# Eight weight-sum jobs moved from batch 1's first passes to batch 0's, the last four token blocks routed singly, and a third buffer for slots and pairs

## The chip, the cores and the metric

The kernel runs on one core of a Trainium2 chip. The metric is the device time of one execution in microseconds (us). The engines are TensorE (PE in the profile; PEld is its weight load), VectorE (DVE), ScalarE (ACT), GpSimd (POOL) and SyncE (SP). GpSimd and SyncE issue the DMAs; each engine works through its own instructions in order.

## The reference

One block of a transformer with modulated norms, on 2 batches of 4096 tokens with 512 channels, in float32: linear attention with 16 heads of 32, then a mixture of 8 experts, of which each token takes 2.

```python
h = layernorm(x) * (1 + ca) + sa
# linear attention: q, k = relu(h @ wq), relu(h @ wk); v with a row of ones
vk  = einsum('bhen,bhdn->bhed', v_pad, k)
out = einsum('bhed,bhdn->bhen', vk, q);  out = out[:-1] / (out[-1:] + EPS)
x = x + ga * (out @ w_proj.T + b_proj)
h = layernorm(x) * (1 + cb) + sb
# experts: top 2 of 8 by softmax of a router; each token's rows are sorted by expert
act = gelu(h_sorted @ w_gate[:, 0]) * (h_sorted @ w_gate[:, 1])
x = x + gb * sum_over_2(weight * (act @ w_linear) * per_expert_scale)
```

## The kernel before, in words

Tokens are worked in blocks of 512 (`TB`), eight per batch, sixteen in all (`order`). There are three stages.

**First passes** (`firsts`, `first`, L907 and L492). For each block the tokens are normed and transposed (`prepare`), then TensorE makes k (`pk`, L500), q (`pq`, L517) and the sum over tokens of k with the normed x (`pa`, L537). VectorE takes each result out of PSUM (L505, L523, L544). The q rows go to DRAM.

**Second passes** (`seconds`, `merge`, `attend`, `second_norm`, L951 on). When a batch's sums are whole, `merge` folds values and projection into one matrix. Then each block reads its q rows back, is divided, transposed and projected (`po`, L682), and normed again (L728, L732). A routed group follows with `route` (L761): VectorE picks the two experts of each token, counts ranks and writes two small tiles, `pair` (token number and weight) and `slot` (the row of the map). GpSimd then scatters them into `map_d` in DRAM, one indirect DMA for 128 tokens and one choice (L887): 16 for a group of two blocks, 8 for one block. `group_of` says which blocks are routed together: two at a time, the last two alone.

**Experts** (L1403 on). Seven products take the place of eight in the big units (`seven`, L1190), for which sums of quarter blocks of the expert weights are wanted beside the weights. The first map fetch (`fetch_map`, L1120) waits for all scatters.

These weight sums are made by the generator `weight_sums` (L419): 24 jobs, two gate halves and one linear weight for each of 8 experts. Each job has four parts:

```python
raw = big(f"wraw_{n}")
nc.gpsimd.dma_start(out=raw..., in_=src)          # L431: 1 MB in, GpSimd's queue
nc.vector.tensor_tensor(to, one, two, op)         # L446: four sums on VectorE
nc.gpsimd.dma_start(out=dst, in_=new...)          # L447: 1 MB out, GpSimd's queue
```

`raw` and `new` are taken from the tag `big`, which has five buffers and is shared with xT of the blocks, h2, and the weights of `merge`.

How the two streams run is written out by hand. All of batch 0's first passes go alone. Then batch 1's first passes and the second passes alternate, six steps of a second pass for each block with two of a first pass behind each. What is left of the second passes goes alone at the end. The framework (Tile) places the instructions on the engines from this order and sets the waits.

Of the kernel before, what the change touches and what calls it, by code (L numbers as in the profile page):

```python
# [10 lines left out]
I32 = mybir.dt.int32  # L11
# [6 lines left out]
P = 128  # L18
B, N, C = 2, 4096, 512
HEADS, HD = 16, 32  # L20
E, TOPK, H = 8, 2, 512
# [7 lines left out]
NBLK = N // TB  # L29
# [21 lines left out]
def adaln_linear_attention_moe_kernel(  # L51
# [81 lines left out]
    with ExitStack() as st:  # L133
# [39 lines left out]
        def load_mod(m):  # L173
            wm = big(f"wm_{m}")
            nc.sync.dma_start(out=wm, in_=chunks(wmod[:, m * C : (m + 1) * C]))
            wm_of[m] = wm
# [39 lines left out]
        def mod_columns(m):  # L216
            wm = wm_of.pop(m)
            pc = bank(f"pmc_{m}")
            for g in range(KC):
                for k in range(KC):  # L220
                    nc.tensor.matmul(
                        pc[:, g * B : (g + 1) * B],
                        wm[:, k, g * P : (g + 1) * P],
                        silu[:, k, :],
                        start=(k == 0), stop=(k == KC - 1),
                    )
            nc.vector.tensor_scalar(
                modc[:, m].rearrange("p k b -> p (k b)"), pc[:, 0 : KC * B],
                float(m == 1), None, ALU.add,
            )  # L230
# [138 lines left out]
        def load_wot():  # L369
            wot_of.append(big("wot"))  # L370
            nc.sync.dma_start(out=wot_of[0], in_=chunks(wprojt))
# [47 lines left out]
        def weight_sums():  # L419

            jobs = []
            for e in range(E):
                rows = slice(e * P, (e + 1) * P)
                for m in range(2):
                    src = wgate[rows, m * 4 * KH * QN : (m + 1) * 4 * KH * QN]
                    r0 = (2 * e + m) * P
                    jobs.append((src, wgsum_d[r0 : r0 + P, :], True))
                jobs.append((wlin[rows, :], wlsum_d[rows, :], False))
            for n, (src, dst, left) in enumerate(jobs):
                raw = big(f"wraw_{n}")  # L430
                nc.gpsimd.dma_start(out=raw.rearrange("p q n -> p (q n)"), in_=src)  # L431
                new = big(f"wnew_{n}")
                a, b, c, d = (raw[:, q, :] for q in range(4))
                s = [new[:, q, :] for q in range(4)]
                if left:
                    steps = (
                        (s[0], d, c, ALU.add), (s[1], s[0], a, ALU.subtract),
                        (s[2], a, d, ALU.subtract), (s[3], b, s[1], ALU.subtract),
                    )
                else:  # L440
                    steps = (
                        (s[0], d, a, ALU.subtract), (s[1], c, s[0], ALU.subtract),
                        (s[2], c, d, ALU.subtract), (s[3], b, s[1], ALU.subtract),
                    )
                for to, one, two, op in steps:
                    nc.vector.tensor_tensor(to, one, two, op)  # L446
                nc.gpsimd.dma_start(out=dst, in_=new.rearrange("p q n -> p (q n)"))  # L447
                yield
# [10 lines left out]
        def prepare(b, i):  # L459

            if (b, i) not in xin:
                load_x(b, i)
            xt = xin[(b, i)]
            name = f"{b}_{i}"
            s6 = sm.tile([P, NT, nc.vector.BN_STATS_DIM], FP, tag="bn6", name=f"bn6_{name}")
            mv = sm.tile([P, NT, 2], FP, tag="mv", name=f"mv_{name}", bufs=4)
            dev = sm.tile([P, NT], FP, tag="dev", name=f"dev_{name}", bufs=4)
            for t in range(NT):
                nc.vector.bn_stats(s6[:, t, :], xt[:, t, :])
                nc.vector.bn_aggr(mv[:, t, :], s6[:, t, :])  # L470
            nc.scalar.activation(dev, mv[:, :, 1], AF.Sqrt, bias=eps_ln)
            nc.vector.reciprocal(mv[:, :, 1], dev)
            t0 = (b * NBLK + i) * NT
            nc.vector.tensor_scalar(xl[:, t0 : t0 + NT, E], mv[:, :, 0], -1.0, None, ALU.mult)
            xh = []
            for t in range(NT):
                h = row("xh", f"xh_{b}_{i}_{t}", 8)
                nc.vector.tensor_scalar(
                    h, xt[:, t, :], mv[:, t, 0:1], mv[:, t, 1:2], ALU.subtract, ALU.mult
                )  # L480
                xh.append(h)
            xT = big(f"xT_{b}_{i}")
            for k in range(KC):
                pt = ps_t.tile([P, 512], FP, tag="tr", name=f"pt_{b}_{i}_{k}")
                for t in range(NT):
                    nc.tensor.transpose(  # L486
                        pt[:, t * P : (t + 1) * P], xh[t][:, k * P : (k + 1) * P], ident
                    )
                nc.scalar.copy(xT[:, k, :], pt)
            prepared[(b, i)] = (xh, xT, dev)  # L490
# [270 lines left out]
        def route(b, group, lm, rq, ssq):  # L761
            blk, nt = group[0], len(group) * NT

            def tl(shape, tag, bufs=1, dt=FP):

                n = 1
                for s in shape[1:]:
                    n *= s
                t = sm.tile([P, n * 2 * NT // nt], dt, tag=tag, name=f"{tag}_{blk}", bufs=bufs)
                t = t[:, 0:n]  # L770
                if len(shape) == 3:
                    return t.rearrange("p (a b) -> p a b", a=shape[1])
                if len(shape) == 4:
                    return t.rearrange("p (a b c) -> p a b c", a=shape[1], b=shape[2])
                return t
# [66 lines left out]
            def chosen(src, tag):  # L842

                prod = tl([P, TOPK, nt * E], "prod")
                nc.vector.tensor_tensor(
                    prod, src, oh.rearrange("p k t e -> p k (t e)"), ALU.mult
                )
                got = tl([P, TOPK, nt], tag)
                nc.vector.tensor_reduce(
                    got, prod.rearrange("p k (t e) -> p k t e", t=nt), AX.X, ALU.add  # L850
                )
                return got

            def over_k(a):
                return a.unsqueeze(1).to_broadcast([P, TOPK, nt * E])
# [18 lines left out]
            nc.vector.tensor_tensor(  # L874
                pk, pk, ren.unsqueeze(1).to_broadcast([P, TOPK, nt]), ALU.mult
            )
            pair = tl([P, TOPK, nt, 2], "pair", 2)
            nc.vector.tensor_tensor(pair[:, :, :, 1], pk, sc, ALU.mult)
            nc.vector.tensor_scalar(
                pair[:, :, :, 0].bitcast(I32), iota_tok[:, :, 0:nt], float(blk * TB), None, ALU.add  # L880
            )
            rank = chosen(over_k(prk), "rank")
            slot = tl([P, TOPK, nt], "slot", 2, I32)
            nc.vector.scalar_tensor_tensor(slot, idx, float(CAP), rank, ALU.mult, ALU.add)  # L884
            for k in range(TOPK):
                for t in range(nt):
# [12 lines left out]
        order = [(b, i) for b in range(B) for i in range(NBLK)]  # L899

        group_of = {}
        for n in range(len(order)):
            alone = n >= len(order) - 2
            group_of[n] = [n] if alone else [n - n % 2, n - n % 2 + 1]
        sums = {}

        def firsts():  # L907

            wsums = weight_sums()
            prepare(0, 0)  # L910
            load_mod(2)
            mod_columns(0)
            load_mod(3)
            mod_columns(1)
            load_mod(5)
            bias_row(0)
            scaled(0, 0)
            for n, (b, i) in enumerate(order):
                if i == 0:
                    sums[b] = (  # L920
                        wp.tile([P, KC, C], FP, tag="acc", name=f"acc_{b}"),
                        wp.tile([P, C], FP, tag="ksum", name=f"ksum_{b}"),
                    )
                steps = first(b, i, *sums[b])
                if n == 0:
                    for _ in range(NT):
                        next(steps)
                        yield
                    bias_row(1)
                    scaled(0, C)  # L930
                    mod_row(4)
                    load_wot()
                    router_columns()
                    for _ in range(NT):
                        next(steps)
                        yield
                    later_rows()
                if n + 1 < len(order):
                    prepare(*order[n + 1])
                if n == 0:  # L940
                    padding()
                if n == 1:
                    for at in (0, C):
                        scaled(1, at)
                for _ in range(2 if b == 0 else 1):
                    next(wsums, None)
                yield from steps

# [539 lines left out]
```

## Time and profile before

| | us |
|---|---|
| median of 3 runs | 2479.77 (2474.09 to 2483.15) |
| profiled execution | 2461.66 |
| its span, first to last instruction | 2459.8 |
| TensorE busy | 2320.4 (94%) |
| VectorE busy | 1466.9 (60%) |
| GpSimd busy | 768.7 (31%) |
| ScalarE busy | 508.7 (21%) |

In the profiled execution batch 0's first passes end at about 416 us, batch 1's at about 927, the last second pass and the routing at about 1135; the experts take the rest. In rows of the profile, "L887" is a line of the kernel, the name after the operation is the tile that is written and behind the arrow what is read. In a timeline the first number is the start, the second the duration, "x8" the number of instructions put together, and the brackets hold the idle time of the engine ahead of the row and what ended it.

### The profile page before, as it was taken

Reading aid. Unit: us, or ns where it says so; the run is one execution under the profiler, and the core shown is the slowest. Engines: PE = TensorE matmul, PEld = TensorE weight load, DVE = VectorE, ACT = ScalarE, POOL = GpSimd, SP = SyncE. Lnnn points to the kernel's source line nnn. Section 1 sums busy time; section 2 is a strip of 40 time slices with the busy share of each in tenths; the row PEclk is TensorE's granted clock in tenths of the full one; section 3 lists DMA queues with packets and bytes.
Section 4 is the critical chain, followed back from the end, with each engine's and each line's share of the span. In section 5 each row is a group of like instructions: output and inputs, shape, how many; then the busy total and the mean of one; then the engine's idle time right before and its main releaser. Section 6 shows DMA issues by size and latency. Waiting matters only on the chain.

```text
span 2459.8 us, 25373 instructions
## 1 busy us (share of the span) xinstructions
PE 2320.4 (94%) x9440; PEld 1681.5 (68%) x9440; DVE 1466.9 (60%) x2895; ACT 508.7 (21%) x1015; POOL 768.7 (31%) x723
## 2 busy tenths in 40 slices
PE   8999999999797999983899999999999999999996
PEld 4565565666464667762777778777887788877884
DVE  3464646666464647994565655655655566655663
ACT  1121211223122323551111111111111111111110
POOL 0100000001102020546544444444544445444431
PEclk9999999999898999996999999999999999999998
DMA  5674544343534534875777777777777777777753
GB/s 210 246 272 145 205 159 159 131 165 116 137 137 125 189 98 126 222 206 167 247 233 240 218 247 231 230 243 254 208 227 234 247 244 213 232 255 222 244 157 66
DMA packets 111728, 486.22 MB, mean 198 GB/s; under 512 B 18593, under 2 KB 18593, under 8 KB 77938
## 3 DMA queue, kind: packets, MB, share of 16 engines
q0 software_dynamic: 71584, 347.12, 45.0%
q1 hardware_dynamic: 40018, 137.44, 17.3%
q8 instruction: 76, 1.25, 0.2%
q14 instruction: 50, 0.41, 0.1%
HBM read 355.63 MB, written 128.88 MB: 197 GB/s over the span
## 4 chain that ended last, share of the span: by engine, by line
PE 83%; DMA 6%; DVE 5%; POOL 4%; issue 2%; ACT 0%; SPq 0%; POOLq 0%; DVEq 0%; ACTq 0%
PE p_g L1200 24%; PE p_l L1200 12%; PE pq L517 9%; PE pgs L1354 8%; PE pa L537 8%; PE pk L500 7%; PE po L682 5%; PE py L1380 4%; POOL map_d L887 3%; DMA map_d<-pair,slot 2%; PE px L1263 2%; DMA x<-in_x 1%; PE pt L486 1%; DMA wraw<-in_wgate 1%; PE pqt L670 1%
## 5 line engine op out<-in xcount | busy, mean ns | idle before, releaser
L1200 PE MATMUL p_g<-xT,wg 128*128 128x256 f32 x1600 | 371.9, 381 | 0.0
L1200 PEld LDWEIGHTS p_g<-xT,wg 128*128 128x128 f32 x1600 | 303.4, 191 | 41.6 <-issue 1.9
L1200 PE MATMUL p_g<-xS,wg 128*128 128x256 f32 x1200 | 283.7, 379 | 0.3 <-DVE xS L1272 0.3
L500 PE MATMUL pk<-wqk,xT 128*128 128x512 f32 x512 | 234.2, 605 | 36.7 <-DVE k L505 36.7
L1200 PEld LDWEIGHTS p_g<-xS,wg 128*128 128x128 f32 x1200 | 228.2, 190 | 31.7 <-DVE xS L1272 1.0
L682 PE MATMUL po<-gm,qT 128*128 128x265 f32 (+1 forms) x1024 | 240.6, 386 | 9.3 <-ACT qT L674 9.3
L517 PE MATMUL pq<-wqk,xT 128*128 128x264 f32 (+1 forms) x1024 | 231.8, 386 | 1.6 <-DVE den L658 1.6
L537 PE MATMUL pa<-k,xh 128*128 128x512 f32 x512 | 225.2, 595 | 0.3 <-DVE acc L544 0.3
L887 POOL DMA_INDIRECT map_d<-pair,slot x128 | 134.2, 1048 | 289.9 <-DVE slot L884 249.1
L517 PEld LDWEIGHTS pq<-wqk,xT 128*128 128x128 f32 x1024 | 195.7, 192 | 37.9 <-issue 4.3
L682 PEld LDWEIGHTS po<-gm,qT 128*128 128x128 f32 x1024 | 189.8, 190 | 44.7 <-ACT qT L674 13.3
L1176 POOL DMA_INDIRECT out<-y_b,mp x100 | 158.1, 1581 | 175.8 <-DVE y_b L1173 152.9
L1354 PE MATMUL pgs<-wgs,xTs 128*128 128x512 f32 x464 | 205.0, 595 | 0.0
L1200 PE MATMUL p_l<-wl,aT 128*128 128x256 f32 x800 | 193.9, 379 | 0.0
L500 PEld LDWEIGHTS pk<-wqk,xT 128*128 128x128 f32 x512 | 95.5, 194 | 142.3 <-issue 100.4
L537 PEld LDWEIGHTS pa<-k,xh 128*128 128x128 f32 x512 | 97.4, 191 | 112.7 <-issue 110.5
L1354 PEld LDWEIGHTS pgs<-wgs,xTs 128*128 128x128 f32 x464 | 88.6, 191 | 111.2 <-issue 109.7
L1200 PEld LDWEIGHTS p_l<-wl,aT 128*128 128x128 f32 x800 | 148.0, 190 | 18.2 <-issue 0.5
L1113 POOL DMA_INDIRECT xg<-h_d,mp x129 | 131.8, 1022 | 71.4 <-issue 34.4
L1292 ACT ACTIVATE ge<-quar_g 128x512 f32<-128x512 f32 x100 | 62.9, 629 | 408.0 <-DVE quar_g L1208 408.0
L1200 PE MATMUL p_l<-wl,aS 128*128 128x256 f32 x600 | 141.8, 379 | 0.0
L1208 DVE TENSOR_TENSOR quar_g<-part_g,p_g 128x512 f32<-128x512 f32 x150 | 102.8, 685 | 53.7 <-PE p_g L1200 51.9
(267 smaller groups left out, 3000.6 us busy)
## 6 DMA issues: line engine op xcount, KB each, us to landing
x<-in_x SPq DMA_DIRECT2D x16, 1024.0 KB
q_d<-q SPq DMA_DIRECT2D x64, 256.0 KB
qi<-q_d SPq DMA_DIRECT2D x64, 256.0 KB
wraw<-in_wgate POOLq DMA_DIRECT2D x16, 1024.0 KB, 6.3
xb_d<-x SPq DMA_DIRECT2D x16, 1024.0 KB
wgsum_d<-wnew POOLq DMA_DIRECT2D x16, 1024.0 KB, 5.6
xb<-xb_d SPq DMA_DIRECT2D x16, 1024.0 KB
out<-xb SPq DMA_DIRECT2D x16, 1024.0 KB
```

The source lines that it names most:

```text
L500: nc.tensor.matmul(pk, xT[:, k, t * P : (t + 1) * P], w[:, k, 0:C], start=(k == 0), stop=(k == KC - 1),)
L517: nc.tensor.matmul(pq[:, C // 2 + c0 : C // 2 + c1], xT[:, k, t * P : (t + 1) * P], w[:, k, C + c0 : C + c1], start=(k == 0), stop=(k == K ...
L537: nc.tensor.matmul(pa, xh[t][:, g * P : (g + 1) * P], ks[t], start=(t == 0), stop=(t == NT - 1),)
L682: nc.tensor.matmul(po[:, C // 2 - EX + c0 : C // 2 - EX + c1], qT[:, g * P : (g + 1) * P], gm[:, g, c0:c1], start=(g == 0), stop=(g == KC ...
L887: ins = nc.gpsimd.indirect_dma_start(out=map_d, out_offset=IndirectOffsetOnAxis(ap=slot[:, k, t : t + 1], axis=0), in_=pair[:, k, t, :], i ...
L1113: return nc.gpsimd.indirect_dma_start(out=dst, out_offset=None, in_=src, in_offset=IndirectOffsetOnAxis(ap=ids, axis=0))
L1176: ins = nc.gpsimd.indirect_dma_start(out=out, out_offset=IndirectOffsetOnAxis(ap=token(mp, t), axis=0), in_=y, in_offset=None, compute_op= ...
L1200: nc.tensor.matmul(bank[:, c, :], left(s, c, k), rhs[:, k, :], start=(k == 0), stop=(k == KH - 1),)
L1208: nc.vector.tensor_tensor(r, one, two, ALU.add)
L1292: nc.scalar.activation(ge, g, AF.Gelu_apprx_tanh)
L1354: nc.tensor.matmul(p, xT[:, k, :], wg[:, :, quarters[k // KH], k % KH, :], start=(k == 0), stop=(k == KC - 1),)
L1380: nc.tensor.matmul(p, aT[:, hc, :], wl[:, q, hc % KH, :], start=(hc == 0), stop=(hc == HC - 1))
```

## The change

Three edits. The weight jobs are taken three per block (`3 * E // NBLK`, which is 3) instead of two per block of batch 0 and one per block of batch 1, so that all 24 are issued with batch 0's eight blocks. The last four blocks are routed singly instead of the last two: blocks 12 and 13, one group with 16 scatters before, become two groups with 8 each. And the tiles `pair` and `slot` have three buffers instead of two.

```diff
-            pair = tl([P, TOPK, nt, 2], "pair", 2)
+            pair = tl([P, TOPK, nt, 2], "pair", 3)
...
-            slot = tl([P, TOPK, nt], "slot", 2, I32)
+            slot = tl([P, TOPK, nt], "slot", 3, I32)
...
         for n in range(len(order)):
-            alone = n >= len(order) - 2
+            alone = n >= len(order) - 4
             group_of[n] = [n] if alone else [n - n % 2, n - n % 2 + 1]
...
                 if n == 1:
                     for at in (0, C):
                         scaled(1, at)
-                for _ in range(2 if b == 0 else 1):
+                for _ in range(3 * E // NBLK):
                     next(wsums, None)
                 yield from steps
```

## The prediction

> **What bounds the kernel now.** I read the page first: its busy line and its two rows in 40 slices.
>
> ```profile
> PE 2320.4 (94%) x9440; PEld 1681.5 (68%) x9440; DVE 1466.9 (60%) x2895; ACT 508.7 (21%) x1015; POOL 768.7 (31%) x723
> ...
> PE   8999999999797999983899999999999999999996
> ...
> PEclk9999999999898999996999999999999999999998
> ```
>
> TensorE works 94% of the span, so time is only to be won where its row dips: slice 10, counted from 0 (615 to 676 us), slice 12 (738 to 799), and slice 18 (1107 to 1168), where the routing ends and the experts begin. Each slice is 61.5 us. The granted clock dips there too.
>
> Next I asked who TensorE waits for from 420 to 1140 us, while batch 1's first passes run beside batch 0's second passes (columns: total us, times, longest):
>
> ```profile
> PE pk L500 <- DVE k L505: 32.8, 2, 18.0
> PE prk L835 <- DVE runs L820: 16.2, 2, 14.2
> PE po L682 <- ACT qT L674: 9.3, 14, 1.0
> ```
>
> Two stalls make 32.8 us. The timelines around them (start, duration, engine, line, in brackets the idle time before) name the cause. GpSimd, 620 to 630 us:
>
> ```profile
> 627.81 0.96 POOL L887 DMA_INDIRECT map_d<-pair,slot  x1 [1.33 <-DMA map_d<-pair,slot]
> 629.45 0.58 POOL L431 DMA_DIRECT2D wraw<-in_wgate  x1 [0.68 <-issue]
> ```
>
> VectorE, then TensorE, 636 to 640 us:
>
> ```profile
> 637.20 1.29 DVE L446 TENSOR_TENSOR wnew<-wraw 128x512 f32<-128x512 f32 x2 [21.29 <-DMA wraw<-in_wgate]
> ...
> 639.02 0.69 DVE L505 TENSOR_TENSOR k<-pk,bias 128x512 f32<-128x512 f32 x1
> ...
> 639.76 5.75 PE L500 MATMUL pk<-wqk,xT 128*128 128x512 f32 x8 [17.99 <-DVE k L505]
> ```
>
> The load of expert weights stands on GpSimd's queue behind the 16 scatters of a routed pair of blocks (603.7 to 628.8 us). VectorE's instruction on it is ahead of the `k` add that frees a PSUM bank, so TensorE stops. At 762 to 777 us the same happens (load issued at 766.27, TensorE idle 14.86).
>
> Last, the end of the routing, GpSimd and VectorE in order of time:
>
> ```profile
> 1091.39 0.96 POOL L887 DMA_INDIRECT map_d<-pair,slot  x1 [16.21 <-DVE slot L884]
> ...
> 1113.96 0.17 DVE L879 TENSOR_SCALAR pair<-iota_tok 128x8 int32<-128x8 f32 x1 [7.16 <-DMA map_d<-pair,slot]
> ...
> 1133.52 0.95 POOL L887 DMA_INDIRECT map_d<-pair,slot  x1 [0.30 <-issue]
> ...
> 1139.11 0.96 POOL L1113 DMA_INDIRECT mp<-map_d,mrowb  x1 [3.34 <-DMA map_d<-pair,slot]
> ```
>
> From 1091.4 to 1134.5 GpSimd issues the last 32 scatters almost without a gap: 16 for blocks 12 and 13, 8 for 14, 8 for 15. The experts' first map fetch waits for all of them. VectorE meanwhile waits 7.16 us for a `pair` buffer.
>
> **The change part by part.**
>
> *Sums leave batch 1.* Eight of the 24 weight jobs ran there. With none left, the two waits have nothing to wait for: 32.8 us. After each stall the first eight matmuls also ran slowly, 5.75 and 5.33 us where eight of the same kind took 3.60 at 758.7 us: 3.9 us more. Sum: 36.7 us gained. What is late next? In the stretches beside the stalls (500 to 560 and 640 to 700 us) TensorE is busy 59.5 to 60.0 of 60 us and VectorE 39 to 40, so nothing else waits close behind. The scatters themselves do not start sooner: at 603.68 they waited for VectorE's slots, not for a load.
>
> *Sums enter batch 0.* Eight blocks get a third job: two GpSimd DMA issues (0.53 us each) and four VectorE sums (0.685 us each, 2.74 together). A steady block shows
>
> ```profile
> 203.38:246.62 43.24, 43.24 (x145) 25.92 (x145) 22.87 (x40) 8.10 (x18) 2.14 (x4) 1.00 0.46 170
> ```
>
> (TensorE, weight loads, VectorE, ACT, GpSimd busy; clock; DMA share; GB/s). VectorE goes from 22.9 to 25.6 of 43.2 us and GpSimd from 2.1 to 3.2, and 2.1 MB more per block bring the DMA from 170 to about 218 GB/s, below the 276 of 100 to 200 us. As busy time all of it is hidden. If TensorE's cover were gone, it would be 22 us of VectorE time.
>
> The risk is order. VectorE works in order, and the loads of a block are taken from five `big` buffers, two of which hold xT. Two loads per block are issued 20 us or more ahead now (at 171.9 and 186.7 for sums at 206.5 and 210.3), and no block from 160 to 416 us has a stall. The third load finds a buffer only when the first sums of its own block are done, so its lead will be short, about 6 to 12 us. The nearest rows are today's short-lead loads: those issued at 85.7, 119.1, 128.3, 423.9 and 835.8 us cost TensorE nothing, the one at 105.2 cost it 3.65 us (VectorE 7.24). Lower end: 0. I exclude a gain, since TensorE is already full there. Upper end: 3.65 us for each of the eight, 29 us. I take 4 us, one such stall, since five rows of six show none and two PSUM banks cover about 3.4 us of a VectorE wait.
>
> A rule of the Trainium skill bears on this. A load takes 6.0 us to land (median; 5.0 to 11.7). "DMA: Bandwidth & Descriptors", section "Anatomy of one DMA — SWDGE (gpsimd) path", gives 2.0 us plus bytes over 436 GB/s, an estimate of 4.4 us here. By the rule every third load lands inside even a 6 us lead, and the term is 0; by the rows it can be over 5 us late, as at 105.2. I go with the rows. Against the change speaks "SBUF — State Buffer", section "Who interferes with whom": a VectorE instruction in a two-port mode locks GpSimd out while it writes descriptors; its page reports a 0.62 us DMA taking 3.1. The 16 moved DMAs, at 2.5 us each, would be an estimate of 40 us of lateness. But the 24 loads' issues, beside the same VectorE work, span only 0.527 to 0.742 us, so I add nothing.
>
> Behind the waits: on GpSimd's queue in batch 0 stand only weight DMAs. On SP's, batch 0's last block has the loads of `wv` and `wo` (issued at 386.5 and 388.1), which need `big` buffers too; these may come up to 16 us later, when xT of block 7 is free at about 402, and 8 us of landing still ends before 418.5, where `wv` is used. The q stores behind them on SP (from 393.5) could then back up to VectorE: 0 to 5 us, and I take 0.
>
> *Last four blocks alone, third buffers.* Block 12's eight scatters (1.27 us apiece from start to start) can go at about 1075, in the idle 16.21 us before 1091.4. Routing costs VectorE more: a pair's route has 35 instructions, listed 7.5 us together; a single one 34, listed 6.5. Starts overlap by about 0.08 us, so the extra route is worth 5.5 - 2.6 = 2.9 us of VectorE time, and VectorE is full there (49.1 of 50 us from 1050 to 1100): 3 us later. On the other side its 7.16 us wait goes. So: slots of block 13 at 1094.0, its scatters to 1104.2; slots of 14 at 1109.5, scatters to 1119.7; slots of 15 at 1123.7 - 7.2 + 3 = 1119.5, scatters to 1129.9 instead of 1134.5. Gain 4.6 us. Ends: 8 us if the extra route hides, 2 if it costs its listed 5.5. Third buffers alone would give nothing: GpSimd has 32 scatters to issue from 1091.4 on whatever VectorE does. They cost only space.
>
> *Sum:* -36.7 + 4 - 4.6 = -37.3 us. It is made against the profiled execution, 2461.7 us (span 2459.8), giving 2424. That execution lies 18.1 us under the median of the three runs (2479.8); I carry the difference over: 2442 us.
>
> **The rivals.**
>
> *The stalls move to batch 0.* Every third load is late by what the one at 105.2 was: +29 instead of +4, net -12, 2467 us. For it: the short lead, and DMA share that rises. Against it: five short-lead loads of six. Chance 0.12, half of it within 0.5%.
>
> *The buffers become the bound (slower).* A job's load, sums and store run one after another through too few `big` buffers, and xT of the next block waits for a store. From 102 to 170 us six stores leave 13.7 us apart, which for three jobs is 41 us per block of 43.2: just inside. At the longest landings (load 11.7, sums 2.7, store 9.5: 24 us) three jobs take 72 us, 29 more per block, 230 over eight: about 2670 us; at 20 us per job +134, about 2570. Loss begins when a job takes over 16.2 us (5.2 us per block, 42 together). Against it: loads and stores of different jobs overlap today (171.9 and 186.7, before the sums at 206). Chance 0.06.
>
> *The stalls are only partly the loads'.* VectorE, freed, stops at the next late thing (q rows from DRAM: 50 us in 21 waits there, all hidden now) or the order of instructions shifts: half of the gain, about 2461 us. Chance 0.10. That the change does not do what it says is unlikely: three times eight calls use up the 24 jobs.
>
> **How the numbers follow.** Main case 0.72: 2442 us. Its own ends (0 to 12 us in batch 0, 2 to 8 at the end, and some 5 us of run spread) give 2430 to 2455; the range up to 2463 takes in the half gain and part of the first rival. About 0.5% (12.4 us) is what a measurement here can tell from no change. Faster: 0.72 + 0.06 + the partial case, less a little for reordering nobody can see here, 0.83. Same 0.09, slower 0.08.
>
> **What would show it.** Right: no weight sums after about 425 us; TensorE's wait on `k` from 420 us on falls from 32.8 to under 3 us; slices 10 and 12 read 9; four groups of eight scatters at the end, no `pair` wait, the first map fetch about 4.6 us nearer to the end of VectorE's last norm. Wrong: waits of `pk` or `pt` on VectorE or on `big` buffers between 100 and 420 us, a block of batch 0 longer than 43.3 us, or a new stall where the two were.

## The result and the profile after

| | before | changed |
|---|---|---|
| median of 8 runs each, us | 2482.5 (2474.1 to 2490.8) | 2462.5 (2460.5 to 2465.7) |
| ratio | | 0.9918, 95% interval 0.9898 to 0.9938 |
| profiled execution, us | 2461.7 | 2465.1 |

The change gains 20 us, 0.8%. The forecast had 37. The two profiled executions alone would show no gain: that of before lay some 20 us under its own median, that of the changed kernel is typical of its runs. Why is told below.

The changed kernel's page, busy line and the two rows in 40 slices:

```profile
PE 2330.3 (95%) x9446; PEld 1688.4 (69%) x9446; DVE 1469.6 (60%) x2928; ACT 511.8 (21%) x1019; POOL 769.4 (31%) x723
...
PE   8999999999899998883899999999999999999996
...
PEclk9999999999899999996999999999999999999998
```

Slice 12 now reads 9, but slice 10 (616 to 677 us) only rose from 7 to 8: something still stands there. Slices 15 and 16 (924 to 1047 us) fell from 9 to 8; they lie in the stage after batch 1, which is longer in this trace (230.0 us instead of 211.3 in the table below). TensorE's waits from 420 to 1135 us, in the order of the view (total us, times, longest):

```profile
PE pq L517 <- DVE den L658: 13.0, 2, 11.3
PE prk L835 <- DVE runs L820: 9.1, 2, 7.1
PE pqt L670 <- issue: 7.8, 5, 4.6
```

The waits of `pk` on `k` (32.8 us before) are gone, and no weight sum runs after 404 us. In their place stands a wait of `pq` on `den`, VectorE's division of a q row, 11.3 us long at 637 us. A q row is loaded from DRAM by SyncE (L651, `qi`) and first used by VectorE at L653 (`qk`).

All stages side by side, from the traces of all runs. "Batch 0" is the time until the first `pks` matmul (L570) that ends batch 0's first passes, "batch 1" from there to the `pks` of batch 1, "end" from there to the first map fetch (`mp<-map_d`, L1113), "experts" the rest of the span. The first two rows are the two profiles that belong to the result; the others are told below; kernels of one set ran together.

| kernel, in us | set | batch 0 | batch 1 | end | experts |
|---|---|---|---|---|---|
| before | - | 416.0 | 511.8 | 211.3 | 1320.7 |
| changed | - | 420.7 | 490.1 | 230.0 | 1322.5 |
| before, second trace | 1 | 419.5 | 514.3 | 213.9 | 1322.4 |
| jobs moved only | 1 | 423.0 | 489.5 | 210.7 | 1322.5 |
| last four alone and third buffers only | 1 | 414.9 | 515.1 | 209.5 | 1322.2 |
| changed, second trace | 1 | 421.3 | 492.6 | 211.9 | 1321.0 |
| changed, without 32 scatters | 2 | 420.1 | 473.2 | 229.6 | 1318.7 |
| jobs early in batch 1 | 2 | 412.9 | 497.1 | 227.0 | 1320.4 |
| every block routed alone | 2 | 425.3 | 489.1 | 223.0 | 1321.7 |
| before, sums' loads on SyncE | 2 | 410.8 | 488.6 | 239.1 | 1320.1 |
| before, third trace | 3 | 413.3 | 512.2 | 234.6 | 1321.6 |
| changed, sums' loads on SyncE | 3 | 457.3 | 486.6 | 237.6 | 1319.8 |
| jobs as before, loads on SyncE, last four alone | 3 | 412.8 | 485.2 | 229.6 | 1319.6 |
| changed, loads on SyncE, every block alone | 3 | 456.6 | 487.4 | 222.9 | 1319.7 |

### The profile page after: what moved, and what is told of

Read it like the earlier page. It is cut to its first block, busy times and chain, and to the rows that moved or that the text cites. A ratio compares the mean times of both kernels' runs of the same rounds, so it can differ in the third digit from the quotient of the medians.

```text
span 2463.3 us, 25420 instructions
## 1 busy us (share of the span) xinstructions
PE 2330.3 (95%) x9446; PEld 1688.4 (69%) x9446; DVE 1469.6 (60%) x2928; ACT 511.8 (21%) x1019; POOL 769.4 (31%) x723
## 3 DMA queue, kind: packets, MB, share of 16 engines
q1 hardware_dynamic: 40018, 137.44, 18.3%
## 5 line engine op out<-in xcount | busy, mean ns | idle before, releaser
L682 PE MATMUL po<-gm,qT 128*128 128x265 f32 (+1 forms) x1024 | 247.9, 394 | 13.1 <-issue 6.1
L1200 PEld LDWEIGHTS p_g<-xS,wg 128*128 128x128 f32 x1200 | 227.9, 190 | 32.8 <-DVE xS L1272 1.8
L500 PE MATMUL pk<-wqk,xT 128*128 128x512 f32 x512 | 228.3, 593 | 2.8 <-DVE k L505 2.8
L517 PEld LDWEIGHTS pq<-wqk,xT 128*128 128x128 f32 x1024 | 196.6, 193 | 49.5 <-issue 18.1
L682 PEld LDWEIGHTS po<-gm,qT 128*128 128x128 f32 x1024 | 193.9, 195 | 50.3 <-issue 10.9
L1200 PEld LDWEIGHTS p_l<-wl,aT 128*128 128x128 f32 x800 | 147.9, 190 | 18.3 <-issue 0.5
L1113 POOL DMA_INDIRECT xg<-h_d,mp x129 | 131.9, 1022 | 72.7 <-issue 34.0
```

Of the source, the lines that this page charges most:

```text
L500: nc.tensor.matmul(pk, xT[:, k, t * P : (t + 1) * P], w[:, k, 0:C], start=(k == 0), stop=(k == KC - 1),)
L517: nc.tensor.matmul(pq[:, C // 2 + c0 : C // 2 + c1], xT[:, k, t * P : (t + 1) * P], w[:, k, C + c0 : C + c1], start=(k == 0), stop=(k == K ...
L682: nc.tensor.matmul(po[:, C // 2 - EX + c0 : C // 2 - EX + c1], qT[:, g * P : (g + 1) * P], gm[:, g, c0:c1], start=(g == 0), stop=(g == KC ...
L1113: return nc.gpsimd.indirect_dma_start(out=dst, out_offset=None, in_=src, in_offset=IndirectOffsetOnAxis(ap=ids, axis=0))
L1200: nc.tensor.matmul(bank[:, c, :], left(s, c, k), rhs[:, k, :], start=(k == 0), stop=(k == KH - 1),)
```

## The experiments

**First set: the parts of the change, and both kernels again.** Jobs only:

```diff
-                for _ in range(2 if b == 0 else 1):
+                for _ in range(3 * E // NBLK):
```

> Three weight jobs per block of batch 0; groups of two and two buffers as in the kernel before. Theory A (all of the gain is the jobs'; a q load that lands late stands behind each stall and keeps about 13 of its 33 us): 2460 to 2466 us, ratio 0.991 to 0.994 to before, last pks at about 911 us, a wait of pq on den of about 11 us near 640. Theory B (the jobs give the full 35 us, and routing four blocks singly gives 13 to 18 back): 2443 to 2448 us, ratio about 0.985.

Measured: 2449.0 us beside 2465.5 for before, ratio 0.9939 (0.9924 to 0.9954). Its waits of TensorE from 420 to 935 us:

```profile
PE pq L517 <- DVE den L658: 13.8, 2, 10.9
```

Theory A: the jobs carry the gain, and a wait on a q row keeps a part of it. The expected absolute time missed, since this set ran about 17 us quicker as a whole, before included; the ratio and the wait hit.

Routing and buffers only:

```diff
-            pair = tl([P, TOPK, nt, 2], "pair", 2)
+            pair = tl([P, TOPK, nt, 2], "pair", 3)
...
-            slot = tl([P, TOPK, nt], "slot", 2, I32)
+            slot = tl([P, TOPK, nt], "slot", 3, I32)
...
-            alone = n >= len(order) - 2
+            alone = n >= len(order) - 4
```

> The last four blocks routed singly and three buffers for pair and slot; the weight jobs as in the kernel before. Theory A (the routing at the end is worth its forecast 4.6 us or nothing): ratio 0.997 to 1.000, the stretch from the last pks to the first map fetch within 5 us of that of an ordinary trace of before. Theory B (routing singly costs): ratio 1.005 to 1.008, that stretch 225 to 232 us.

Measured: 2463.7 us, ratio 0.9996 (0.9985 to 1.0008): no difference that can be measured, and surely no cost of 13 us. What it does to the end is seen in GpSimd's rows, the first scatter of each of the last three blocks (13, 14 and 15), the last scatter of all and the map fetch:

```profile
1098.14 1.22 POOL L887 DMA_INDIRECT map_d<-pair,slot  x1 [10.91 <-DVE slot L884]
...
1112.96 0.96 POOL L887 DMA_INDIRECT map_d<-pair,slot  x1 [3.96 <-DVE pair L878]
...
1124.19 1.14 POOL L887 DMA_INDIRECT map_d<-pair,slot  x1 [0.58 <-DVE iota_jb L116]
...
1133.52 0.96 POOL L887 DMA_INDIRECT map_d<-pair,slot  x1 [0.30 <-issue]
...
1139.42 0.96 POOL L1113 DMA_INDIRECT mp<-map_d,mrowb  x1 [3.65 <-DMA map_d<-pair,slot]
```

The last `pks` stood at 929.9 us here and at 927.8 in the first trace of before, so the last scatter came 203.6 us after it instead of 205.7: 2 us won. Beside the trace of before from its own set the whole end is 4.4 us shorter (209.5 and 213.9 us).

The kernel before and the changed one, unchanged, for second traces:

> The kernel before, unchanged, for a second trace. Its first profiled execution (2461.7 us) was some 20 us quicker than its timed runs, the changed kernel's (2465.1) is typical of its own. Theory A (the first trace was a quick execution, and what the ordinary runs lose lies in the second passes that run alone at the end): this trace is near 2480 us, the sums' two stalls are there again (wait of pk on k about 33 us from 420 to 1140 us), and the stretch from the last pks matmul to the first map fetch is 220 to 230 us instead of 211. Theory B (the changed kernel's order makes that stretch longer): this trace has 209 to 213 us there, and the 20 us are elsewhere, in the experts (over 1335 us instead of 1321).

> The changed kernel, unchanged, for a second trace and beside the other two. Theory A: ratio 0.990 to 0.994; the wait of pq on den near 640 us is there again within 2 us of 11.3, since it has a fixed cause (a q load issued behind the stores of the block, landing beside the scatters), while the small gaps of TensorE beside the scatters at the end (963 to 1072 us) may be fewer or more. Theory B (both are chance): one of them is absent and the run is 10 us or more quicker.

Measured: before 2471.8 us in its profiled execution, with the two stalls again (34.4 us, longest 18.3) and an end of 213.9 us, so theory A's 220 to 230 was a miss there, as was theory B's over 1335 us for the experts (1322.4). The changed kernel: ratio 0.9917 (0.9902 to 0.9931), the wait of `pq` on `den` again, longest 10.9 us, and an end of 211.9 us instead of 230. So the gain is repeatable, the new wait has a fixed cause, and the long end of the first changed trace has not: the same program in the same order took 18 us less there.

**Second set: what the q row waits for.** The second trace of the changed kernel, SyncE, VectorE and TensorE in order of time around the wait:

```profile
618.71 0.32 SPq L552 DMA_DIRECT2D xb_d<-x  x1
623.68 0.32 SPq L651 DMA_DIRECT2D qi<-q_d  x1
636.64 0.33 SPq L162 DMA_DIRECT2D x<-in_x  x1
639.11 0.69 DVE L653 TENSOR_TENSOR qk<-qi,kall 128x512 f32<-128x512 f32 x1 [14.45 <-DMA qi<-q_d]
648.92 6.56 PE L517 MATMUL pq<-wqk,xT 128*128 128x256 f32 x16 [10.93 <-DVE den L658]
655.95 0.32 SPq L651 DMA_DIRECT2D qi<-q_d  x1
659.22 0.69 DVE L653 TENSOR_TENSOR qk<-qi,kall 128x512 f32<-128x512 f32 x1 [3.02 <-DMA qi<-q_d]
```

A q row is usually used 3.2 us after its load was issued (655.95 to 659.22). The one at 623.68 took 15.4 us. The scatters of the first group run from 609 to 634 us. The store `xb_d` ahead of it is slow as well: the load of `x` behind it waits for its landing and goes only 17.9 us later.

The first experiment leaves out the scatters of blocks 0 to 3, so these tokens' rows are missing from the map, and it was run once, for its trace; the order on all other queues is the same instruction by instruction:

```diff
-            for k in range(TOPK):
+            for k in range(TOPK if blk >= 4 else 0):
                 for t in range(nt):
                     ins = nc.gpsimd.indirect_dma_start(
```

> The changed kernel with the scatters of blocks 0 to 3 left out (32 of 128 indirect DMAs; the map rows of these tokens keep their padding, so the experts work on padding rows there), everything else in the same order. It asks what holds up the q load near 624 us, whose first VectorE instruction waits 14 us. Theory A (the packets of the 16 scatters): the wait of pq on den falls from 13 to 14 us to under 2, VectorE's wait on the q load to about 3, and batch 1's first passes (last pks to last pks) take 477 to 480 us instead of 490 to 493. Theory B (the three transfers of 1 MB issued ahead of it on the same queue): the wait stays at 8 us or more.

Its rows in the same place:

```profile
616.89 0.32 SPq L552 DMA_DIRECT2D xb_d<-x  x1
621.85 0.32 SPq L651 DMA_DIRECT2D qi<-q_d  x1
622.26 0.38 SPq L162 DMA_DIRECT2D x<-in_x  x1
625.55 0.69 DVE L653 TENSOR_TENSOR qk<-qi,kall 128x512 f32<-128x512 f32 x1 [2.71 <-DMA qi<-q_d]
```

The store lands within 5.4 us, the q row is used after 3.7, and no wait of `pq` on `den` is left among TensorE's waits. Batch 1 takes 473.2 us instead of the changed kernel's 490.1 and 492.6. Theory A. What the scatters do to the transfers is seen in the table of stretches (two of 12 us, the changed kernel's second trace first, then without scatters; the last three columns are clock, DMA share, GB/s):

```profile
612.00:624.00 12.00, 11.85 (x44) 6.08 (x43) 8.79 (x13) 3.85 (x9) 9.56 (x9) 1.00 0.70 138
624.00:636.00 12.00, 12.00 (x44) 7.67 (x43) 0.66 (x1) 0.90 (x2) 5.38 (x6) 1.00 0.80 149
```

```profile
610.00:622.00 12.00, 12.00 (x43) 6.10 (x43) 8.83 (x13) 4.01 (x10) 0.00 (x0) 1.00 0.67 262
622.00:634.00 12.00, 12.00 (x43) 7.60 (x42) 9.19 (x23) 3.21 (x6) 0.00 (x0) 1.00 0.42 132
```

With about the same DMA share (0.70 and 0.67), the engines move 138 GB/s beside scatters and 262 without. The view of the DMA queues divides this up (packets, MB, share of the 16 engines' time; q0 has GpSimd's transfers, q1 SyncE's), with scatters and without:

```profile
q1 hardware_dynamic: 217, 1.65, 67.9%
q0 software_dynamic: 145, 0.00, 1.6%
```

```profile
q1 hardware_dynamic: 432, 3.15, 66.6%
```

The scatters' own packets take only 1.6% of the engines' time. SyncE's transfers hold the engines for as long as without them and move half the bytes: each of their packets takes about twice as long. By what means the scatters slow them is not shown. In the second stretch of 12 us the DMA share is 0.80 where it would be 0.42, and VectorE works 0.66 us where it would work 9.19.

Next, the loads of the kernel before moved off the queue of the scatters:

```diff
-                nc.gpsimd.dma_start(out=raw.rearrange("p q n -> p (q n)"), in_=src)
+                nc.sync.dma_start(out=raw.rearrange("p q n -> p (q n)"), in_=src)
```

> The kernel before, with the loads of the weight sums (not their stores) issued on SyncE's queue instead of GpSimd's. Theory A (the load was late because it stood behind 16 scatters on GpSimd's queue): the wait of pk on k falls from 33 to 35 us to the 11 to 14 us that the q load costs there anyway; ratio 0.990 to 0.994. Theory B (it was late because the DMA engines were busy with the scatters, whatever queue it is issued on): the waits stay at 25 us or more, ratio 0.997 to 1.002. In between: SyncE's queue, which works in order, is itself held by the load's wait for a buffer, and stores behind it come late: some new wait.

Measured: 2461.0 us beside 2487.1, ratio 0.9884 (0.9858 to 0.9910). All 24 jobs are where before has them. TensorE's waits from 420 to 935 us:

```profile
PE pq L517 <- DVE lm L691: 6.8, 3, 5.5
PE pk L500 <- DVE k L505: 3.7, 2, 2.5
```

The two stalls are gone, as theory A has it: 3.7 us of them are left, and with the new waits of `pq` on `lm` 10.5 us, near the 11 to 14 that it expected. The load near the first stall, and the sum that uses it:

```profile
600.10 0.42 SPq L431 DMA_DIRECT2D wraw<-in_wgate  x1
614.44 1.29 DVE L446 TENSOR_TENSOR wnew<-wraw 128x512 f32<-128x512 f32 x2 [5.08 <-DMA wraw<-in_wgate]
```

The first scatters of this kernel are issued from 597 us on, so the load goes out among them instead of behind the last (629.45 us in the trace of before, whose scatters began at 603.68). It is slow there, 14.3 us to its use, and the q row issued at 611.81 takes 13.6 us; but both come so early that TensorE's two waits there are 2.5 and 5.5 us instead of 18.0. So the stalls came from the place behind 16 scatters on GpSimd's queue. This one line gains what the whole change gains or more (the intervals overlap from 0.990 to 0.991, and the two kernels did not run in one set), without moving a job. That also batch 0 came out at 410.8 us, the shortest of all traces, was not expected; VectorE's and SyncE's instructions are ordered differently from its start on, so queue and order are not told apart there.

The same from the other side: two jobs per block in batch 0 as before, and four in each of batch 1's first two blocks, all ahead of the first scatter.

```diff
-                for _ in range(3 * E // NBLK):
+                for _ in range(2 if b == 0 else 4):
```

> The changed kernel, with two weight jobs per block of batch 0 as before, and four in each of batch 1's first two blocks, whose loads all come before the first scatters at about 608 us. Theory A (what the jobs cost in batch 1 was their place behind the scatters, nothing else): batch 0's first passes end at 415 to 418 us instead of 421, batch 1's take 490 to 493, ratio to before 0.989 to 0.991. Theory B (the sums cost in batch 1 whatever their place, since VectorE also has the second passes there): batch 1's take 500 us or more and the ratio is 0.995 or higher.

Measured: 2458.8 us, ratio 0.9880 (0.9859 to 0.9900). Batch 0 lost nothing (412.9 us), batch 1 took 497.1: between the two theories for the stage, with the ratio of A or better. The sums cost little in batch 1 (6.4 us more than the 490.7 of the changed order) so long as no scatter stands ahead of their load; the q row is late here too (issued at 624.50, used at 631.60), with waits of `pq` on `den` of 9.6 us.

Shorter bursts, with every block routed alone:

```diff
-            alone = n >= len(order) - 4
+            alone = True
```

> The changed kernel with every block routed singly, so bursts of 8 scatters instead of 16. Theory A (the q load is held up for as long as a burst lasts): a burst of 8 holds it up half as long, and TensorE has some 3 us of cover, so its waits on den fall from 13.8 to 3 to 7 us; six routes more on VectorE are hidden; ratio to before 0.987 to 0.990. Theory B (each burst costs the same, or VectorE's extra routes show): there are twice as many, the waits from 420 to 1140 us grow, ratio 0.993 or higher.

Measured: 2458.9 us, ratio 0.9880 (0.9858 to 0.9902), as theory A has it, but not by its mechanism. Each late q row is late for less, as it says: used 6.3 to 9.6 us after its issue, where the two of the changed kernel took 15.4 and 8.3. But there are four of them now, so the waits on `den` are 10.5 us in four times instead of 13.8 in two, not the 3 to 7 that were expected, and batch 1 took 489.1 us, hardly less than the changed kernel. The end took 223.0 us where the changed kernel's order gave 227 to 230 in this set. Whether it is quicker than the changed kernel at all stays open; they did not run in one set.

**Third set: the two cures together.** The changed kernel with its sums' loads on SyncE's queue, and the same with every block alone:

> The changed kernel with the loads of the weight sums on SyncE's queue. Batch 0's first passes should end at 411 to 417 us instead of 421 (they did at 411 with the loads on SyncE's queue and two jobs per block). Theory A (moving the jobs adds something beyond the queue): batch 1's first passes take 490 to 493 us as in the changed kernel, and the ratio to before is 0.985 or less. Theory B (with the loads on the quick queue, the place of the jobs is of no account): the ratio is that of the next kernel within 0.2%.

> The changed kernel with the loads of the weight sums on SyncE's queue and every block routed singly. Each alone gave 0.988 (the latter with the changed kernel, the former with the kernel before). Theory A (they remove different losses: the start of batch 0, and half of each q load's lateness): ratio 0.982 to 0.986. Theory B (what they remove is the same, or the q loads stay late by as much in sum): ratio 0.987 to 0.990.

Measured: 2498.3 us, ratio 1.0039 (1.0025 to 1.0052), and 2488.0, ratio 1.0001 (0.9991 to 1.0011). All these theories fell (the "next kernel" of the first text is the one with the jobs as before, told last, at 0.9852): batch 0 now takes 457 us instead of 421. Of the first of the two kernels, what TensorE and VectorE wait for most between 160 and 457 us as far as it bears on this, and its SyncE queue in one block (in the row of the q stores, "17.20" is the time over which four were issued):

```profile
PE pq L517 <- ACT xl L526: 23.5, 6, 4.9
```

```profile
DVE wnew L446 <- DMA wraw<-in_wlin: 25.0, 6, 5.1
```

```profile
182.28 17.20 SPq L532 DMA_DIRECT2D q_d<-q  x4
199.57 0.39 SPq L431 DMA_DIRECT2D wraw<-in_wgate  x1
...
215.27 0.38 SPq L431 DMA_DIRECT2D wraw<-in_wgate  x1
...
228.59 0.33 SPq L431 DMA_DIRECT2D wraw<-in_wlin  x1
```

The same three loads on GpSimd's queue, in the changed kernel's second trace:

```profile
188.70 0.53 POOL L431 DMA_DIRECT2D wraw<-in_wgate  x1
194.89 0.53 POOL L431 DMA_DIRECT2D wraw<-in_wgate  x1 [5.66 <-DMA wlsum_d<-wnew]
...
219.53 0.55 POOL L431 DMA_DIRECT2D wraw<-in_wlin  x1
```

SyncE works in order, and the block's first load stands behind four q stores, each of which waits for its q: it goes at 199.57 instead of 188.70. The third load is then 9 us later too. In six blocks VectorE reaches its sums before it has landed and stops, with the q adds queued behind, and behind these ACT's `xl`, the last reader of TensorE's bank: 25.0 us of VectorE's waits, 23.5 of TensorE's, and slow matmuls after each (16 of `pq` took 6.69 us after the wait at 190.90). A block takes 49 to 54 us instead of 43.25 (its first `pt` at 157.57, the next at 211.16 and 260.35). This is the stall that the prediction feared for GpSimd's queue, brought about by standing behind other work on SyncE's.

So the jobs go where they were, their loads on SyncE's queue, and the last four blocks alone:

> The weight jobs where the kernel before has them (two per block of batch 0, one per block of batch 1), their loads on SyncE's queue, and the last four blocks routed singly with three buffers. The run with the loads on SyncE's queue alone lost 20.6 us in one wait of TensorE for the routing (prk on runs) at the end; routed singly this wait is 7 us. Theory A (that wait is on the path): ratio 0.982 to 0.986, better than 0.988. Theory B (it is not, since the experts wait for VectorE's and GpSimd's last work): ratio 0.987 to 0.990.

Measured: 2449.7 us beside 2489.2, ratio 0.9852 (0.9838 to 0.9865), the ratio of theory A. It is the lowest of all versions, and its interval does not meet those of the changed kernel's 0.9917 and 0.9918, which were taken in other sets. Batch 0 took 412.8 us, batch 1 485.2. That the wait of `prk` is on the path is not shown by it: the longest such wait did fall, from 20.6 to 7.1 us, but the two ends, 239.1 and 229.6 us, are of different sets, and batch 1 was 3.4 us shorter too.

A third trace of before ran beside these:

> The kernel before, unchanged, a third trace, on the chip of the next three. The stretch from the last pks matmul of batch 1 to the first map fetch took 211 and 214 us in two traces of it and 210 to 212 in three others of the second one's set, but 223 to 239 us in the four traces of the set after that (kernels derived from the changed one or from before) and 230 in the first trace of the changed kernel. Theory A (the machine's state sets it, whatever the kernel): it is here as long as in the next three traces, short or long, within 10 us. Theory B (the kernels that run quicker in batch 1 lose it there): it is 211 to 214 us here, and 222 or more in the next three.

Measured: an end of 234.6 us, 2483.5 in all. The others of this set took 222.9 to 237.6 for the end. Theory A in the main, though one of the three lies 11.7 us away where it allowed 10: the same kernel has an end of 211 us in one trace and of 235 in another. The three sets ran on three different chips, one each, so that chip and moment are not told apart. Where the end was long, its rows show waits whose end the profile does not explain (`issue`: it shows nothing that was waited for; `remote`: it does not show who ended the wait); in the third trace of before, from 926 to 1165 us:

```profile
PE po L682 <- issue: 15.8, 6, 6.3
...
ACT qT L674 <- remote: 19.4, 3, 8.2
```

In the second trace of before, with the end of 213.9 us, no wait of `po` of this kind is listed. What holds the engines there stays open.

## Why the prediction was right, and where its sum was wrong

The range (2430 to 2463) held the time, 2462.5, by half a microsecond, and the direction was right. The likeliest case, 2442, was not what happened: it came out as the third rival had it, half of the gain, 2461. The range reached that far to take in half of the gain, a size that was not worked out; that it was just wide enough is luck. Of the signs that it named, those for right came (no sums after 404 us, the wait on `k` and the wait for `pair` gone), and one for wrong too: a new stall where the first of the two had been.

**Sums leave batch 1: forecast -36.7 us, measured -22.6.** Four traces with one job per block in batch 1, their loads behind the scatters, took 511.8, 514.3, 512.2 and 515.1 us for batch 1, 513.4 in the mean; three with the jobs in batch 0 and blocks 0 to 11 routed in pairs took 490.1, 492.6 and 489.5, mean 490.7. The stalls went as forecast. The step that failed is the clause "so nothing else waits close behind". It was argued from the stretches beside the stalls. But the scatters that held the weight load back on GpSimd's queue also slow what SyncE has in flight beside them, and the q row issued at 618.36 us in the trace of before was one of these: it was used at 640.82, right behind the sums' wait, which covers whatever lateness of its own it had. Without the sums it shows: 13.8 us of waits, plus the slow matmuls after the longer one (6.56 us where 16 of the kind took 3.67), 2.9: 16.7 us. Without scatters as well, batch 1 takes 473.2 us, 17.6 less, which is that sum within 1 us, and 40 us less than before: about the 36.7 was there to be had, but not by moving the jobs alone. The rival named the q rows from DRAM as the next late thing and gave it a chance of 0.10; its size was "half of the gain", not worked out.

**Sums enter batch 0: forecast +4 us (0 to 29), measured +5.4.** Batch 0 took 416.0, 419.5, 413.3 and 414.9 us with two jobs per block (mean 415.9), and 420.7, 421.3, 423.0 and 420.1 with three (mean 421.3). The three traces of before alone differ by 6 us, and with the two further orders of the table (412.9 with two, 425.3 with three) the difference is 6.8. From 160 to 421 us TensorE waits for nothing in the changed kernel, as before; all of it is lost at the start. The rows name the place: a block of `x` that SyncE loads, VectorE's first use of it, and TensorE's `pa`, which waits for an `acc` add behind that. Before, then the changed kernel's second trace:

```profile
137.31 0.36 SPq L162 DMA_DIRECT2D x<-in_x  x1
146.25 1.29 DVE L469 BATCH_NORM_STATS2 bn<-x 128x6 f32<-128x512 f32 x2 [3.20 <-DMA x<-in_x]
149.50 7.13 PE L537 MATMUL pa<-k,xh 128*128 128x512 f32 x16 [0.32 <-DVE acc L544]
```

```profile
142.54 0.33 SPq L162 DMA_DIRECT2D x<-in_x  x1
153.07 1.28 DVE L469 BATCH_NORM_STATS2 bn<-x 128x6 f32<-128x512 f32 x2 [6.45 <-DMA x<-in_x]
156.81 5.11 PE L537 MATMUL pa<-k,xh 128*128 128x512 f32 x8 [4.05 <-DVE acc L544]
```

The wait of `pa` on `acc` is 3.7 to 7.1 us in all five traces with three jobs per block and the loads on GpSimd's queue. With two jobs it is 0.3 us or less in four of five; the second trace of before has 3.9, behind a block of `x` that VectorE waited 6.8 us for. So the loss is a late block of `x`, not the late weight load for which the forecast set its 4 us: that the two numbers are close is luck. What makes the block late beside the third job was not tested. Of the two prices for a load, the row was the nearer one: 18 loads whose landing the changed kernel's second trace tells took 7.4 us in the median (5.6 to 9.8), where the Trainium skill's formula ("DMA: Bandwidth & Descriptors", section "Anatomy of one DMA — SWDGE (gpsimd) path") came to 4.4; before's second trace has 7.1, so the third job did not bring this. VectorE waited for only two of the 24 loads, 7.9 us together; in batch 0 before it was one, 7.2 us. The lock-out of GpSimd shows nowhere: the issues still take 0.53 us in the median. The rival of the stalls moving to batch 0 is out. That of the buffers as the bound is out too: no load was late enough to stop TensorE after 160 us, until the loads were put behind the q stores on SyncE's queue.

**Last four alone, third buffers: forecast -4.6 us (2 to 8), measured -1 (-3.7 to +2.0) as that part alone, and -4.3 (-9.1 to +0.5) on top of the moved jobs.** The second figure is the mean of the changed kernel's five runs in the first set less that of the six with the jobs alone. Neither is clear of nothing. The order of events is the forecast one: VectorE's wait for `pair` is gone, block 13's scatters begin 168.2 us after the last `pks` (166.2 forecast, counted from 927.8) and 14's at 183.0 (181.7 forecast). Block 15's begin at 194.3 instead of 191.7; VectorE was later than worked out, and 2 us of the 4.6 were left against that trace. Within the first set the end is 4.4 us shorter with this part alone and 1.2 us longer on top of the moved jobs (211.9 and 210.7). TensorE's wait of `prk` on `runs` fell from 16.2 to 9.0 us; no gain of that size shows in the time. In the sets with the long end, orders with the last four alone took 227 to 238 us and those with pairs 234.6 and 239.1. That points to a few us more there, but no pair of timed runs in one of these sets tells it.

**The 18.1 us carried over.** The forecast took the difference between before's profiled execution and its median as common to both kernels. The third trace of before shows where such a difference can lie: in the end (234.6 us instead of 211.3), while batch 0, batch 1 and the experts agree within 3 us. The routing edits bear on the end, so it was not sure to be common to both. It came out so: the parts as measured in the traces add up to about what the medians show.

The sum as it was measured: -22.6 + 5.4 - 1 = -18.2 us against -20 in the medians.

## What to carry to other kernels

When a wait ends on a transfer that is late, ask why it is late before you count the wait as won: what delays one transfer may delay others in flight beside it, and a second late one stands unseen behind the first. Look up, in the trace of before, the next instruction on that engine that needs a transfer, when it was issued and whether the hidden time would have been enough. And before moving work away from a busy queue, try moving only its DMA to another queue; there, count what stands ahead of it and what that waits for.

## What was not expected of the hardware

A scatter DMA of 128 tokens moves almost no bytes, but with 16 of them in 25 us the DMA engines moved about half as much for the others in one stretch (138 instead of 262 GB/s), with 1.6% of their time spent on the scatters' own packets; and a q row of 256 KB took 15.4 us instead of 3.2 to its use. And the stretch at the end, with scatters, stores and three engines at work, took 211 or 235 us for the very same program in different traces, with waits of TensorE and ACT that the profile does not explain; a kernel's single trace should be set beside its own timed runs before two traces are compared.
